# Attention in units of eight slots: scores and maxima in one stretch, projection and rotation behind it, then the unit's own values

## Chip, cores, metric

The kernel runs on one core of a Trainium2 chip. The metric is the device time of one execution in microseconds; of several runs the median counts. The engines are TensorE (PE; its weight loads are PEld), VectorE (DVE), ScalarE (ACT), GpSimd (POOL) and SyncE (SP), which here issues all DMAs. TensorE writes into eight PSUM banks, each of 128 partitions x 512 floats.

## What is computed

A layer of three parts over x of shape (4, 1024, 128): half a routed feed-forward network of eight experts, attention with low-rank query and key paths, and half the same feed-forward network again.

```python
def _reference_tuple_inner(x, w_down_q, w_down_kv, w_up_q, w_up_k, w_up_v, w_out, ln_scale, ln_bias):
    b, s, d = x.shape
    residual = x
    h = (x - mu) * jax.lax.rsqrt(var + LN_EPS) * ln_scale + ln_bias
    c_q = h @ w_down_q.T
    c_kv = h @ w_down_kv.T
    q = (c_q @ w_up_q.T).reshape(b, s, H, DH).transpose(0, 2, 1, 3)
    k = (c_kv @ w_up_k.T).reshape(b, s, H, DH).transpose(0, 2, 1, 3)
    v = (c_kv @ w_up_v.T).reshape(b, s, H, DH).transpose(0, 2, 1, 3)
    q = _apply_rope_subspace(q, DR)
    k = _apply_rope_subspace(k, DR)
    scores = jnp.einsum('bhqd,bhkd->bhqk', q, k) * scale
    attn = jax.nn.softmax(scores, axis=-1)
    out = jnp.einsum('bhqk,bhkd->bhqd', attn, v)
    out = out.transpose(0, 2, 1, 3).reshape(b, s, H * DH)
    out = out @ w_out.T + residual
...
x = x + 0.5 * _L0_ffn_ref(_layernorm(x, axis=-1), ...)
x = x + _L0_attn_ref(_layernorm(x, axis=-1), ...)
x = x + 0.5 * _L0_ffn_ref(_layernorm(x, axis=-1), ...)
```

There are 16 heads of 64. The indices of the top scores are not part of the result.

## The kernel before

**Stages.** The first feed-forward part runs to about 240 us, attention to about 1493 us, then the second feed-forward part. The change lies in the attention loop, in `run`.

**Units and slots.** A pair of heads and half of a batch's queries (512) make a *unit*; there are 64. A unit has eight *slots*, one for each block of 128 keys, 512 slots in all (`NSLOT`). The loop goes over 128 groups of four slots (`NGRP`), and one more to finish.

**Scores.** `score` (L769) makes one slot's scores for one head in four matmuls: three for the product in split precision, the fourth subtracts the row maxima, which stand in `maxr`. Both heads of the pair run next to each other, in the upper and lower 64 rows of the array. The bank is chosen in L779 from five, psS[0] to psS[3] and psX. After the fourth matmul ACT writes the exponential into a tile `p` (L785), of which there are `PBUFS` = 8, and POOL adds the unit's tiles up in `acc` (`accumulate`, L797); `direct` says how many of the last tiles TensorE sums instead.

**Maxima.** `passA` (L744) makes unsplit scores in psA[0] or psA[1] (one for each head), and DVE reduces them (L756). It runs 15 slots ahead (`AHEAD`). `MAXIMA` says before which score of a group each maxima stand. After a unit's sixteenth reduction `max_row` sends the maxima through DRAM to a row.

**Values.** `values` (L799) multiplies the `p` tiles of a slot with the latents `ckn` into psC, in sixteen matmuls for a group; at the unit's last slot ACT copies psC to `osb` (L806). A group does the values of the group before it.

**Denominators and projection.** `den` (L808) sums `acc` over partitions into a bank from `aux`, copies it, and sends it through DRAM to `dT`. `outp` (L827) multiplies `osb` with the folded matrix `G` in banks `bankO` (psX and psS[3]), one bank for each head; `add` in it scales head 0 on ACT (L849), scales and adds head 1 on DVE (L852), and adds head 0 (L854).

**Rotation.** `rope` (L625) makes queries and keys of later pairs in nine stages: fetch the latents, six matmuls into psX and psS[3] ("mm"), five DVE operations ("vector", L660 to L664), two casts on ACT (L672), a subtraction on POOL (L680), two DMAs out.

**Background.** Generators for the next batch's normalization and routing give one step at a time: `step` takes the next whose kind (other, VectorE, TensorE) is allowed at that place. Their PSUM banks come from `aux`, which goes round `rest`: psS[0] and psS[1].

**Order.** The schedule is manual: each engine executes its instructions in the order in which the program makes them. Within a group: the pairs of scores and maxima of both heads in turn; at the tenth pair the due DMAs and a background step; then the matmuls in `halves` (a projection in one group, a rotation in the next), the denominators every second group, the rotation's DVE work, due work ("end"), loads of later pairs, the casts, and the values of the group before, with a background step after the second slot. `at` puts work under a group and a place, `run_later` does it there. All DMAs of the loop stand in SP's queue in the order of issue.

Of the kernel before, what the change touches and what calls it, by code (L numbers as in the profile page):

```python
# [27 lines left out]
AHEAD = 15  # L28
NSLOT = B * 128
NGRP = NSLOT // 4  # L30
PBUFS = 8
MAXIMA = ((3, 8, 13), (0, 5, 10))
OTHER, VECTOR, PE, NEVER = 0, 1, 2, 3
NROPE = 9
ACTS = (4, 6, 7)
# [5 lines left out]

def direct(U):

    return 1 if U % 3 == 2 and U < 56 else 0


class Kernel:
# [494 lines left out]
    def attn_pre(self, b):  # L542
# [15 lines left out]
        def stage(k, h):  # L558
# [30 lines left out]
            elif k in (far[6], far[6] + 1):  # L589
                if k == far[6]:  # L590
                    st["y2", h] = rows4(new("ya2", 2))
                self.norm(st["y2", h], [y[:, i, :] for i in range(4)], mv2[:, q], rstd2[:, q], k - far[6])
            elif k == far[7]:
                ps = self.aux()
                for i in range(4):
                    nc.tensor.transpose(ps[:, i * 128:(i + 1) * 128], st["y2", h][:, i, :], self.ident)
                st["hT", h] = new("hT_a", 0)
                nc.scalar.activation(st["hT", h], ps, AF.Identity, bias=self.lnsb[:, 1:2], scale=self.lnsb[:, 0:1])
            elif k == far[8]:

                pc = self.aux()
                nc.tensor.matmul(pc, self.wdn, st["hT", h], start=True, stop=True)
                st["ckT", h] = new("ckT", 3)[0:64]
                nc.scalar.copy(st["ckT", h], pc[0:64, :])
                C = st["C", h] = self.prep.tile([128, 2, 512], F32R, name="C_a", bufs=2)
                nc.vector.tensor_copy(C[:, 0, :], pc)
                nc.vector.tensor_tensor(C[:, 1, :], pc, self.f(C[:, 0, :]), ALU.subtract)
            elif k == far[8] + 1:
                self.dma(out=self.c_scr[b][h], in_=st["C", h])
                self.latents.add((b, h))  # L610
            elif k == far[9]:
                assert b < 2 or self.slot > 128 * (b - 1)
                pt = self.aux()
                for i in range(4):
                    nc.tensor.transpose(pt[:, i * 64:(i + 1) * 64], st["ckT", h][:, i * 128:(i + 1) * 128], self.ident[0:64, 0:64])
                nc.vector.tensor_copy(self.ckn[b % 2][:, 4 * h:4 * h + 4, :], pt[:, 0:256].rearrange("p (t l) -> p t l", t=4))

        for k in range(far[9] + 1 + far[10]):
# [6 lines left out]
    def rope(self, n, stage):  # L625
# [29 lines left out]
        elif stage == "vector":  # L655
# [4 lines left out]
            nc.vector.tensor_tensor(rt[:, 0:2, :], even.unsqueeze(1).to_broadcast([128, 2, 512]), self.table[:, 1:3, cs], ALU.mult)  # L660
            nc.vector.tensor_tensor(even, odd, self.table[:, 0, cs], ALU.mult)
            nc.vector.tensor_tensor(odd, odd, self.table[:, 1, cs], ALU.mult)
            nc.vector.tensor_tensor(w["eo"][:, 1, :], odd, rt[:, 1, :], ALU.add)  # L663
            nc.vector.tensor_tensor(w["eo"][:, 0, :], even, rt[:, 0, :], ALU.add)  # L664
        elif stage == "sum":
# [133 lines left out]
    def values(self, s):  # L799
        nc = self.nc  # L800
        U, c = divmod(s, 8)
        b = U // 16
        for hh in range(2):
            nc.tensor.matmul(self.psC[64 * hh:64 * hh + 64, :], self.ckn[b % 2][:, c, :], self.p_of[s][:, hh, :], start=c == 0, stop=c == 7)  # L804
        if c == 7:
            nc.scalar.copy(self.osb_of.pop(U), self.psC)  # L806

    def den(self, U):  # L808

        nc = self.nc  # L810
        osb = self.osb_of[U] = self.op2.tile([128, 512], F32, name="osb")
        pd = self.aux()
        parts = [self.p_of[8 * U + c] for c in range(8 - direct(U), 8)] + [self.acc_of[U]]
        for k, part in enumerate(parts):
            for n in range(4):
                nc.tensor.matmul(pd[32 * n:32 * n + 32, 0:256], self.ones, part[:, n // 2, 256 * (n % 2):256 * (n % 2) + 256], start=k == 0, stop=k == direct(U))  # L816
# [6 lines left out]
        last = U == 2 * 8 * B - 1  # L823
        self.at(self.group + 1, lambda: nc.sync.dma_start(out=dT, in_=d1.rearrange("(h x) (y p) -> p (h x y)", x=2, p=128)), "mid")
        self.at(self.group + (4 if last else 3), lambda: self.outp(U, osb, dT), "side")

    def outp(self, U, osb, dT):  # L827

# [27 lines left out]
        self.at(self.group, add)  # L856

    def run(self):
# [4 lines left out]
        self.ready, self.routed, self.done, self.roped, self.latents = set(), set(), set(), set(), set()  # L863
        streams = [[], [], []]

        credit = [0.0] * len(streams)
# [144 lines left out]
        def rope(g, place):  # L1011
            for d, stages in ROPE[place].items():
                n, r = divmod(g - d, 2)
                if r == 0 and 0 <= n and n + NROPE < 16 * B:
                    for stage in stages.split():
                        self.rope(n + NROPE, stage)

        for g in range(NGRP + 1):
            s0 = 4 * g
            self.group, self.slot = g, s0  # L1020
            rope(g, "side")
            self.run_later(g, "side")

            def rows(hh):
                maxima = lambda i: self.passA(s0 + AHEAD + i, hh) if s0 + AHEAD + i < NSLOT else None
                for n in range(16):
# [9 lines left out]
            side = self.halves  # L1038
            for n, pair in enumerate(zip_longest(rows(0), rows(1))):
                for fn in pair:  # L1040
                    if fn:
                        fn()
                if n == 9:
                    rope(g, "mid")
                    self.run_later(g, "mid")
                    step(OTHER)
            self.halves = [[], []]
# [6 lines left out]
            free = g < 16 or g % 2 == 1 or g >= 2 * (16 * B - NROPE) + 2  # L1054
            step(PE if free else OTHER, free)
            if g and g % 2 == 0:
                self.den(g // 2 - 1)
            rope(g, "end")
            self.run_later(g, "end")
            if g == 1 or (g < NGRP and g % 4 == 3):  # L1060
                P = g // 4 + 3 if g > 1 else 2
                if P < NP:
                    for n, fn in enumerate(self.loads(P)):
                        self.at(g + 1 + n // 8, fn, ("mid", "end")[n // 4 % 2])
                if P == NP + 1:
                    self.ffn_weights2(self.QT[a], self.KT[a], self.QT[c])
                    self.dma(out=xs[0], in_=self.x2_scr[0])

            rope(g, "cast")
            for s in range(s0 - 4, s0):  # L1070
                if s >= 0:
                    self.values(s)
                if s == s0 - 3:
                    step(VECTOR, free)
        for i in range(2):
            for k in range(2):
                for hl in range(2):
# [4 lines left out]
        with ExitStack() as ctx:  # L1082
# [5 lines left out]
            g = self.ffn_pre(self.prep, (6, 7), x_of, self.wts2[:, 3].rearrange("p e t -> p t e"), rows=3)  # L1088

            def bg2(n):  # L1090
                for place in ("mid", "side", "end"):
                    self.run_later(NGRP + 1 + n, place)
                    self.both()
                if n >= GS:
# [59 lines left out]
```

## Time and profile before

| what | value |
| --- | --- |
| runs before | 1653.92, 1653.47, 1652.03 us; median 1653.47 |
| span of the profiled execution | 1648.4 us |
| TensorE matmul instructions | 11044 |
| score matmuls into psS / psX (L781, with the row of maxima) | 3584 / 512 |
| values (L804) | 2048 instructions, 468.8 us busy, 600 ns each |
| maxima on DVE (L756) | 1024, 684.8 us busy, 688 ns each |
| exponentials on ACT (L785) | 1024, some 600 ns each |
| sums on POOL (L797) | 430, 872.6 + 152.4 us busy, 2.38 us each |
| copies of psC (L806) | 64, the first at 253.4 us, the last at 1493.0 us |

The copies of psC mark the units: (1493.0 - 253.4)/63 = 19.7 us from one to the next. In a group of instructions the page gives the line, the engine, what it writes and reads, how often, then the time in which at least one was running, the mean length of one, and the idle time of the engine just before. Matmuls overlap one another, so their lengths do not add up; from start to start is the better measure. In the timeline the columns are start, length, engine, line and operation, and in brackets the engine's idle time before and what ended it.

### The profile page before, as it was taken

To read this page: it belongs to the slowest core of one execution; us is meant where nothing else is said; L and a number is where in the kernel's file an instruction comes from. 1 tells how busy PE (TensorE), PEld (TensorE's weight loads), DVE (VectorE), ACT (ScalarE), POOL (GpSimd) and SP (SyncE) were. 2 spreads that over 40 slices of the span, in tenths; PEclk is the share of its full clock that TensorE was granted. 3 is DMA by queue.
4 is the path that set the end of the run, shared out by engine and by line. 5 is a ranking of instruction groups with operands and counts; after the bars stand their busy time and mean duration, and the time that the engine had idled before them with its cause. 6 is when DMAs were issued, how large, how long until landed. Compare 5 with 4: busy or idle time off the path is not lost.

```text
span 1648.4 us, 31237 instructions
## 1 busy us (share of the span) xinstructions
PE 1593.2 (97%) x11044; PEld 1033.2 (63%) x11044; DVE 1317.6 (80%) x2417; ACT 1013.5 (61%) x2220; POOL 1456.0 (88%) x833
## 2 busy tenths in 40 slices
PE   7998989999999999999999999999999999998998
PEld 5876765566566665666565666666566655656776
DVE  6556668888988888888899889889988868616897
ACT  4675666666666666666666656666566655654555
POOL 5668889999999989999999999999999999895676
PEclk9999999999999999999999999999999999999999
DMA  7025557555555655555555556666655532114443
GB/s 226 1 65 166 155 141 168 142 142 130 134 140 140 142 142 134 146 140 138 131 138 142 129 143 152 150 147 141 141 140 149 130 66 53 36 57 138 140 133 103
DMA packets 241149, 212.28 MB, mean 129 GB/s; under 512 B 157664, under 2 KB 170592, under 8 KB 240224
## 3 DMA queue, kind: packets, MB, share of 16 engines
q1 hardware_dynamic: 240992, 210.28, 50.6%
q8 instruction: 87, 1.43, 0.4%
q14 instruction: 70, 0.57, 0.1%
HBM read 130.39 MB, written 79.82 MB: 128 GB/s over the span
## 4 chain that ended last, share of the span: by engine, by line
PE 68%; POOL 3%; DVE 3%; ACT 2%; issue 2%; POOLq 0%; DVEq 0%; ACTq 0%
PE psc L804 24%; PE ps_s L781 21%; PE ps_a L755 6%; PE psx L781 3%; PE ps_s L521 3%; PE ps_s L816 2%; PE psx L476 2%; PE psx L839 2%; POOL acc L797 2%; PE psx L647 2%; ACT p L785 1%; PE ps_s L839 1%; POOL p L529 1%; PE psc L521 1%; DVE m L756 1%
## 5 line engine op out<-in xcount | busy, mean ns | idle before, releaser
L797 POOL TENSOR_TENSOR acc<-acc,p 128x1024 f32<-128x1024 f32 x366 | 872.6, 2384 | 56.3 <-ACT p L785 30.8
L756 DVE TENSOR_REDUCE m<-ps_a 128x1 f32<-128x512 f32 x1024 | 684.8, 688 | 158.0 <-PE ps_a L755 136.2
L785 ACT ACTIVATE p<-ps_s 128x512 f32<-128x512 f32 x896 | 478.2, 602 | 230.7 <-PE ps_s L781 197.1
L781 PE MATMUL ps_s<-QT,KT 64*128 64x512 f32 x2688 | 548.3, 397 | 3.1 <-DVE eo L663 3.0
L804 PE MATMUL psc<-p,ckn 128*64 128x512 f32 x2048 | 468.8, 600 | 0.0
L781 PEld LDWEIGHTS ps_s<-QT,KT 64*128 64x128 f32 x2688 | 351.2, 185 | 138.8 <-issue 76.3
L755 PE MATMUL ps_a<-KT,QT 64*128 64x512 f32 x1024 | 417.9, 419 | 5.0 <-DVE m L756 3.5
L804 PEld LDWEIGHTS psc<-p,ckn 128*64 128x64 f32 x2048 | 135.8, 137 | 257.3 <-issue 252.3
L781 PE MATMUL ps_s<-maxr,one_row 64*128 64x512 f32 x896 | 237.0, 391 | 0.0
L755 PEld LDWEIGHTS ps_a<-KT,QT 64*128 64x128 f32 x1024 | 184.5, 184 | 36.4 <-DVE m L756 12.8
L797 POOL TENSOR_TENSOR acc<-p 128x1024 f32<-128x1024 f32 x64 | 152.4, 2381 | 14.2 <-ACT p L785 11.9
L806 ACT COPY osb<-psc 128x512 f32<-128x512 f32 x64 | 37.6, 587 | 193.3 <-PE psc L804 193.3
L680 POOL TENSOR_TENSOR eo<-eo,hi_r 128x1024 fp32r<-128x1024 f32 x55 | 132.0, 2400 | 0.0
L781 PEld LDWEIGHTS ps_s<-maxr,one_row 64*128 64x128 f32 x896 | 122.3, 185 | 13.5
L781 PE MATMUL psx<-QT,KT 64*128 64x512 f32 x384 | 110.2, 393 | 0.0
L529 POOL TENSOR_TENSOR p<-eo,p 128x512 fp32r<-128x512 f32 x42 | 62.7, 1499 | 40.6 <-ACT p L528 33.1
L425 POOL TENSOR_TENSOR X<-X,dtmp 128x512 f32<-128x512 f32 x54 | 69.1, 1280 | 32.1 <-ACT dtmp L424 31.0
L852 DVE SCALAR_TENSOR_TENSOR X<-ps_s,rT,X 128x128 f32<-128x128 f32 x248 | 68.8, 339 | 26.4 <-PE ps_s L839 26.4
L849 ACT ACTIVATE psx<-psx,rT 128x128 f32<-128x128 f32 x248 | 85.4, 344 | 6.0
L672 ACT CAST hi_r<-eo 128x512 fp32r<-128x512 f32 x128 | 72.9, 615 | 18.8 <-POOL eo L667 14.0
L785 ACT ACTIVATE p<-psx 128x512 f32<-128x512 f32 x128 | 76.9, 601 | 4.4 <-issue 2.1
L781 PEld LDWEIGHTS psx<-QT,KT 64*128 64x128 f32 x384 | 71.1, 185 | 8.5
(237 smaller groups left out, 2388.2 us busy)
## 6 DMA issues: line engine op xcount, KB each, us to landing
C_l<-cs SPq DMA_DIRECT2D x128, 256.0 KB
QT<-qs SPq DMA_DIRECT2D x256, 128.0 KB
KT<-ks SPq DMA_DIRECT2D x256, 128.0 KB
qs<-hi_r SPq DMA_DIRECT2D x32, 512.0 KB
qs<-eo SPq DMA_DIRECT2D x32, 512.0 KB
ks<-hi_r SPq DMA_DIRECT2D x32, 512.0 KB
ks<-eo SPq DMA_DIRECT2D x32, 512.0 KB
rt<-wt SPq DMA_DIRECT2D x52, 256.0 KB
```

The costliest lines, as they stand in the source:

```text
L425: nc.gpsimd.tensor_tensor(X[:, t:t + 4, :], X[:, t:t + 4, :], tmp, ALU.add)
L529: (nc.gpsimd if m < N - 1 else nc.vector).tensor_tensor(sh[:, 1, :], hp, self.f(sh[:, 0, :]), ALU.subtract)
L672: nc.scalar.copy(w["hi"][:, k, :], w["eo"][:, k, :])
L680: nc.gpsimd.tensor_tensor(w["eo"].bitcast(F32R), w["eo"], self.f(w["hi"]), ALU.subtract)
L755: nc.tensor.matmul(self.psA[hh], self.QT[P % 3][r, 0, q0:q0 + 128], self.KT[P % 3][r, 0, kk * 512:kk * 512 + 512], start=True, stop=True)
L756: nc.vector.tensor_reduce(m[0][:, hh, qb, kk:kk + 1], self.psA[hh], AX.X, ALU.max)
L781: nc.tensor.matmul(ps, w, x, start=k == 0, stop=k == 3)
L785: nc.scalar.activation(self.p_of[s][:, hh, :], ps, AF.Exp, scale=0.125)
L797: nc.gpsimd.tensor_tensor(acc, self.p_of[s - 1] if c == 1 else acc, self.p_of[s], ALU.add)
L804: nc.tensor.matmul(self.psC[64 * hh:64 * hh + 64, :], self.ckn[b % 2][:, c, :], self.p_of[s][:, hh, :], start=c == 0, stop=c == 7)
L849: nc.scalar.activation(po[0][:, c], po[0][:, c], AF.Identity, scale=rT[:, i:i + 1])
L852: nc.vector.scalar_tensor_tensor(x, po[1][:, i * 128:(i + 1) * 128], rT[:, 4 + i:5 + i], x, ALU.mult, ALU.add)
```

## The change

The loop goes over 64 units of eight slots instead of 128 groups of four. In a unit:

- Scores and maxima of eight slots stand in one stretch, with new positions in `MAXIMA`. Background steps of kind "other" stand at the pairs 9, 17 and 26 of it, due DMAs at 9, 17 and 26.
- Behind it come the matmuls of the projection and then those of the rotation (`halves`), with the last maxima between them. `bankO` is now psS[1] and psS[2]; the rotation keeps psX and psS[3].
- Then the projection's scaling (both heads on ACT, "scale"), the denominators of the unit before (`den`, in psS[0]), the casts of the rotation before, the DVE work of this rotation, the projection's two sums on DVE, the rotation's sums, its DMAs.
- Then the values of this unit's own eight slots, with background steps after the second, fourth and sixth, and one step that may use TensorE (two in the first eight units). `rest`, the banks for these steps, is now psA.
- `PBUFS` is 10 instead of 8; `direct` is 3 for the last unit, so that TensorE sums its last three tiles. After the loop the last unit's denominators follow.
- The DMA scratch is set to 1024 bytes. L779, which picks a score's bank, is as before.

```diff
-PBUFS = 8
-MAXIMA = ((3, 8, 13), (0, 5, 10))
+NUNIT = NSLOT // 8
+PBUFS = 10
+MAXIMA = ((2, 8, 13, 19, 24, 29), (0, 5, 11, 16, 21, 27))
...
-    return 1 if U % 3 == 2 and U < 56 else 0
+    return 3 if U == NUNIT - 1 else 1 if U % 3 == 2 and U < 56 else 0
...
         if c == 7:
-            nc.scalar.copy(self.osb_of.pop(U), self.psC)
+            osb = self.osb_of[U] = self.op2.tile([128, 512], F32, name="osb")
+            nc.scalar.copy(osb, self.psC)
...
-        pd = self.aux()
+        pd = self.psS[0]
...
+        g = 2 * U + 4
+        self.at(g + (U == NUNIT - 1), lambda: nc.sync.dma_start(out=dT, in_=d1.rearrange("(h x) (y p) -> p (h x y)", x=2, p=128)), "mid")
+        self.at(g + (3 if U == NUNIT - 2 else 2 if U == NUNIT - 1 else 1), lambda: self.outp(U, self.osb_of.pop(U), dT), "side")
...
-            for i in range(4):
-                c = slice(i * 128, (i + 1) * 128)
-                nc.scalar.activation(po[0][:, c], po[0][:, c], AF.Identity, scale=rT[:, i:i + 1])
-            for i in range(4):
-                x = self.X[:, t0 + i, :]
-                nc.vector.scalar_tensor_tensor(x, po[1][:, i * 128:(i + 1) * 128], rT[:, 4 + i:5 + i], x, ALU.mult, ALU.add)
             x = self.X[:, t0:t0 + 4, :]
-            nc.vector.tensor_tensor(x, po[0].rearrange("p (t d) -> p t d", t=4), x, ALU.add)
-
+            for hh in range(2):
+                nc.vector.tensor_tensor(x, po[hh].rearrange("p (t d) -> p t d", t=4), x, ALU.add)
+
+        def scale():
+            for hh in range(2):
+                for i in range(4):
+                    c = slice(i * 128, (i + 1) * 128)
+                    nc.scalar.activation(po[hh][:, c], po[hh][:, c], AF.Identity, scale=rT[:, 4 * hh + i:4 * hh + i + 1])
+
+        self.at(self.group, scale, "scale")
...
-        self.rest, self.rope_banks, self.bankO = self.psS[:2], [self.psX, self.psS[3]], [self.psX, self.psS[3]]
+        self.rest, self.rope_banks, self.bankO = self.psA, [self.psX, self.psS[3]], self.psS[1:3]
...
-        ROPE = {"mid": {2: "dhi"}, "side": {0: "mm"}, "end": {-1: "fetch", 0: "vector", 2: "dlo"}, "cast": {1: "hi0 hi1 lo"}}
+        ROPE = {"mid": {2: "dlo"}, "side": {0: "mm"}, "vector": {0: "vector"}, "add": {0: "add"}, "cast": {1: "hi0 hi1 lo"}, "end": {1: "dhi", -1: "fetch"}}
...
+        for U in range(NUNIT):
+            s0 = 8 * U
+            self.group, self.slot = 2 * U, s0
...
+                for n in range(32):
                     if n in MAXIMA[hh]:
                         yield lambda n=n: maxima(MAXIMA[hh].index(n))
-                    yield lambda n=n: self.score(s0 + n // 4, hh, n % 4) if g < NGRP else None
+                    yield lambda n=n: self.score(s0 + n // 4, hh, n % 4)
                 if hh == 1:
-                    yield lambda: maxima(3)
-                yield from side[hh]
-                if hh == 0:
-                    yield lambda: maxima(3)
+                    yield lambda: maxima(6)
+                for n, fn in enumerate(side[hh]):
+                    if hh == 0 and n == 2:
+                        yield lambda: maxima(6)
+                    yield fn
...
+                yield lambda: maxima(7)
...
                 if n == 9:
-                    rope(g, "mid")
-                    self.run_later(g, "mid")
+                    self.run_later(2 * U, "mid")
                     step(OTHER)
+                if n == 17:
+                    rope(U, "mid")
...
+                    self.run_later(2 * U, "end")
+                    step(OTHER)
+                if n == 26:
+                    self.run_later(2 * U + 1, "mid")
+                    step(OTHER)
+                if n == 32:
+                    self.run_later(2 * U + 1, "side")
+                    rope(U, "side")
...
+            self.run_later(2 * U + 1, "scale")
+            if U:
+                self.den(U - 1)
+            rope(U, "cast")
+            rope(U, "vector")
+            self.run_later(2 * U + 1, "end")
+            rope(U, "add")
+            rope(U, "end")
+            for k in range(8):
+                self.values(s0 + k)
+                if k in (1, 3, 5):
+                    step(VECTOR if k == 5 or U < 8 else OTHER)
             self.nrest = 0
...
+            for _ in range(2 if U < 8 else 1):
+                step(PE)
+        self.run_later(NGRP, "mid")
+        self.den(NUNIT - 1)
```

More of the change, by code (lines that the diff above doesn't have):

```diff
@@ L615, in stage @@
                     nc.tensor.transpose(pt[:, i * 64:(i + 1) * 64], st["ckT", h][:, i * 128:(i + 1) * 128], self.ident[0:64, 0:64])
+                self.keys.add((b, h))
                 nc.vector.tensor_copy(self.ckn[b % 2][:, 4 * h:4 * h + 4, :], pt[:, 0:256].rearrange("p (t l) -> p t l", t=4))
@@ L662, in rope @@
             nc.vector.tensor_tensor(odd, odd, self.table[:, 1, cs], ALU.mult)
+        elif stage == "add":
+            (even, odd), rt = w["ps"], self.rt
             nc.vector.tensor_tensor(w["eo"][:, 1, :], odd, rt[:, 1, :], ALU.add)
@@ L802, in values @@
         b = U // 16
+        assert (b, c // 4) in self.keys
         for hh in range(2):
@@ L805, in values @@
         if c == 7:
-            nc.scalar.copy(self.osb_of.pop(U), self.psC)
+            osb = self.osb_of[U] = self.op2.tile([128, 512], F32, name="osb")
+            nc.scalar.copy(osb, self.psC)
     def den(self, U):
         nc = self.nc
-        osb = self.osb_of[U] = self.op2.tile([128, 512], F32, name="osb")
-        pd = self.aux()
+        pd = self.psS[0]
         parts = [self.p_of[8 * U + c] for c in range(8 - direct(U), 8)] + [self.acc_of[U]]
@@ L815, in den @@
             for n in range(4):
-                nc.tensor.matmul(pd[32 * n:32 * n + 32, 0:256], self.ones, part[:, n // 2, 256 * (n % 2):256 * (n % 2) + 256], start=k == 0, stop=k == direct(U))
+                nc.tensor.matmul(pd[32 * n:32 * n + 32, 0:256], self.ones, part[:, n // 2, 256 * (n % 2):256 * (n % 2) + 256], start=k == 0, stop=k == len(parts) - 1)
         dsb = self.op1.tile([128, 256], F32, name="dsb")
@@ L822, in den @@
         nc.sync.dma_start(out=d1, in_=dsb[0:128:32, :])
-        last = U == 2 * 8 * B - 1
-        self.at(self.group + 1, lambda: nc.sync.dma_start(out=dT, in_=d1.rearrange("(h x) (y p) -> p (h x y)", x=2, p=128)), "mid")
-        self.at(self.group + (4 if last else 3), lambda: self.outp(U, osb, dT), "side")
+        g = 2 * U + 4
+        self.at(g + (U == NUNIT - 1), lambda: nc.sync.dma_start(out=dT, in_=d1.rearrange("(h x) (y p) -> p (h x y)", x=2, p=128)), "mid")
+        self.at(g + (3 if U == NUNIT - 2 else 2 if U == NUNIT - 1 else 1), lambda: self.outp(U, self.osb_of.pop(U), dT), "side")
     def outp(self, U, osb, dT):
@@ L862, in run @@
         self.later, self.m_of, self.acc_of, self.p_of, self.osb_of, self.rope_of = {}, {}, {}, {}, {}, {}
-        self.ready, self.routed, self.done, self.roped, self.latents = set(), set(), set(), set(), set()
+        self.ready, self.routed, self.done, self.roped, self.latents, self.keys = set(), set(), set(), set(), set(), set()
         streams = [[], [], []]
@@ L1006, in step, with rope @@
             return OTHER
-        ROPE = {"mid": {2: "dhi"}, "side": {0: "mm"}, "end": {-1: "fetch", 0: "vector", 2: "dlo"}, "cast": {1: "hi0 hi1 lo"}}
-        def rope(g, place):
+        ROPE = {"mid": {2: "dlo"}, "side": {0: "mm"}, "vector": {0: "vector"}, "add": {0: "add"}, "cast": {1: "hi0 hi1 lo"}, "end": {1: "dhi", -1: "fetch"}}
+        def rope(U, place):
             for d, stages in ROPE[place].items():
-                n, r = divmod(g - d, 2)
-                if r == 0 and 0 <= n and n + NROPE < 16 * B:
+                if 0 <= U - d and U - d + NROPE < 16 * B:
                     for stage in stages.split():
[L1016 to L1022, printed above, removed]
+                        self.rope(U - d + NROPE, stage)
+        for U in range(NUNIT):
+            s0 = 8 * U
+            self.group, self.slot = 2 * U, s0
+            self.halves = [[], []]
+            side = self.halves
             def rows(hh):
                 maxima = lambda i: self.passA(s0 + AHEAD + i, hh) if s0 + AHEAD + i < NSLOT else None
-                for n in range(16):
+                for n in range(32):
                     if n in MAXIMA[hh]:
                         yield lambda n=n: maxima(MAXIMA[hh].index(n))
-                    yield lambda n=n: self.score(s0 + n // 4, hh, n % 4) if g < NGRP else None
+                    yield lambda n=n: self.score(s0 + n // 4, hh, n % 4)
                 if hh == 1:
-                    yield lambda: maxima(3)
-                yield from side[hh]
-                if hh == 0:
-                    yield lambda: maxima(3)
-            side = self.halves
+                    yield lambda: maxima(6)
[3 more added lines that the diff above has]
+                    yield fn
+                if hh == 0 and len(side[hh]) < 3:
+                    yield lambda: maxima(6)
+                yield lambda: maxima(7)
             for n, pair in enumerate(zip_longest(rows(0), rows(1))):
@@ L1043, in run @@
                 if n == 9:
-                    rope(g, "mid")
-                    self.run_later(g, "mid")
+                    self.run_later(2 * U, "mid")
                     step(OTHER)
+                if n == 17:
+                    rope(U, "mid")
+                    if U % 2 == 0:
+                        P = U // 2 + 2
+                        if P < NP:
+                            for k, fn in enumerate(self.loads(P)):
+                                self.at(2 * U + (k // 4 + 1) // 2, fn, ("end", "mid")[k // 4 % 2])
+                        if P == NP + 1:
+                            self.ffn_weights2(self.QT[a], self.KT[a], self.QT[c])
+                            self.dma(out=xs[0], in_=self.x2_scr[0])
+                    self.run_later(2 * U, "end")
[6 more added lines that the diff above has]
+                    rope(U, "side")
             self.halves = [[], []]
@@ L1051, in run @@
                 streams[1].append(pre2(b - 1))
-            self.nrest = 0
[L1054 to L1074, printed above, removed]
+            self.run_later(2 * U + 1, "scale")
[10 more added lines that the diff above has]
+                    step(VECTOR if k == 5 or U < 8 else OTHER)
+            self.nrest = 0
+            for _ in range(2 if U < 8 else 1):
+                step(PE)
+        self.run_later(NGRP, "mid")
+        self.den(NUNIT - 1)
         for i in range(2):
@@ L1090, in bg2 @@
             def bg2(n):
-                for place in ("mid", "side", "end"):
+                for place in ("mid", "side", "scale", "end"):
                     self.run_later(NGRP + 1 + n, place)
@@ L1149 @@
     x = _layout({n: np.asarray(v) for n, v in inputs.items()})
-    nc = bacc.Bacc("TRN2", target_bir_lowering=False, num_devices=1)
+    nc = bacc.Bacc("TRN2", target_bir_lowering=False, num_devices=1, dynamic_dma_scratch_size=1024)
     build(nc)
```

## The prediction

> **What bounds the kernel now.** I read the page's busy shares and its chain first, then the attention stage's busy times, then who makes TensorE wait there, then TensorE's timeline of one unit, then all engines around one change of work. The page and its chain:
>
> ```profile
> PE 1593.2 (97%) x11044; PEld 1033.2 (63%) x11044; DVE 1317.6 (80%) x2417; ACT 1013.5 (61%) x2220; POOL 1456.0 (88%) x833
> ...
> PE 68%; POOL 3%; DVE 3%; ACT 2%; issue 2%; POOLq 0%; DVEq 0%; ACTq 0%
> ```
>
> The changed loop runs from 240 to 1493 us, busy times in the order PE, PEld, DVE, ACT, POOL:
>
> ```profile
> 240.00:1493.00 1253.00, 1238.39 (x9166) 751.90 (x9163) 1037.14 (x1886) 779.30 (x1654) 1176.95 (x547) 1.00 0.54 129
> ```
>
> TensorE works 98.8% of it at full granted clock; POOL stands at 94%, 76 us short. TensorE's waits in that window are (total, times, longest):
>
> ```profile
> PE ps_s L816 <- POOL acc L797: 5.9, 1, 5.9
> PE psx L647 <- ACT p L785: 2.7, 8, 1.1
> PE ps_a L755 <- DVE m L756: 2.2, 5, 0.8
> PE psx L839 <- ACT p L785: 1.5, 5, 0.5
> ```
>
> Some 12 us in 64 units. So the end is set by TensorE's own issue; every microsecond for which its queue is held lengthens the run, and what leaves its queue shortens it. One unit, TensorE alone (start, length):
>
> ```profile
> 1126.72 0.50 PE L781 MATMUL ps_s<-QT,KT 64*128 64x512 f32 x1
> ...
> 1127.06 0.63 PE L781 MATMUL ps_s<-QT,KT 64*128 64x512 f32 x4
> ...
> 1131.22 0.27 PE L839 MATMUL psx<-G,osb 64*128 64x128 f32 x1
> ...
> 1132.44 3.65 PE L804 MATMUL psc<-p,ckn 128*64 128x512 f32 x16
> 1136.02 0.50 PE L781 MATMUL ps_s<-QT,KT 64*128 64x512 f32 x1
> ...
> 1142.12 0.64 PE L816 MATMUL ps_s<-acc,ones 128*32 128x256 f32 x8
> 1142.68 3.66 PE L804 MATMUL psc<-p,ckn 128*64 128x512 f32 x16
> ```
>
> The two heads run side by side, so I count ticks, one for a pair. A half unit has 16 ticks of scores and 3 of maxima before its projection: from the second tick (1127.06) to the projection (1131.22) are 18 ticks in 4.16 us, 0.231 each. The first takes 0.34, because it follows another kind of work. Four slots of values run 3.58 us to the next score (1132.44 to 1136.02). Last, a half where TensorE must wait for an exponential, all engines:
>
> ```profile
> 700.01 0.40 PE L781 MATMUL ps_s<-maxr,one_row 64*128 64x512 f32 x2
> ...
> 700.50 2.07 ACT L785 ACTIVATE p<-ps_s 128x512 f32<-128x512 f32 x4 [3.23 <-PE ps_s L781]
> ...
> 703.20 0.61 ACT L785 ACTIVATE p<-psx 128x512 f32<-128x512 f32 x1
> ...
> 703.68 1.59 ACT L785 ACTIVATE p<-ps_s 128x512 f32<-128x512 f32 x3
> ...
> 703.86 0.50 PE L647 MATMUL psx<-C_l,wup 64*128 64x512 f32 x1 [0.21 <-ACT p L785]
> ...
> 704.20 0.39 PE L647 MATMUL psx<-C_l,wup 64*128 64x512 f32 x1
> ```
>
> Four prices: a slot's first exponential starts 0.49 after its last score matmul (700.01 to 700.50) and takes 0.60; the next follows after 0.48 (703.20 to 703.68); the bank's next writer starts 0.05 after the end (703.81 to 703.86); and after such a wait the second tick comes 0.34 later instead of 0.23, so a restart costs 0.11.
>
> **The change, part by part.**
>
> *One stretch of eight slots.* It does not touch L779: a score's bank is still (2(s mod 4)+head) mod 5. In order, slots 0 to 7 write banks 0,1 | 2,3 | 4,0 | 1,2 | 0,1 | 2,3 | 4,0 | 1,2. Five banks would allow a distance of five; from slot 3 to slot 4 it is three. Before, 3.58 us of values stood between these slots. Now slot 4 follows at once. Let T be the start of slot 3's last matmuls (both heads at tick 18). Head 0's exponential runs from T+0.49 to T+1.09 and frees bank 1 at T+1.14; slot 4's head 1 wants it two ticks after T, at T+0.46 (maxima fill its place in the tick between). Bank 0, due at T+0.23, is free by T+0.46, since slot 2 ended four ticks before; that lies within the same wait. TensorE's queue is in order, so behind the held matmul stand all later scores and maxima, and DVE and POOL behind those. The loss is 1.14 - 0.46 = 0.68, with the restart 0.79. Bounds: 0.5 if ACT's start is quicker, 1.6 if a pair of normalizations (0.78 in ACT's queue) comes just before; such pairs I price apart. 64 units x 0.79 = 51 us.
>
> *Projection right after the stretch, in banks 1 and 2.* These (psS[1:3]) are the banks of slot 7, the last written. T' is its last tick. The projection's head 0 is due at T'+0.23 and gets its bank at T'+1.14: 0.91, plus the restart 0.11. Head 1's bank comes free at T'+0.49+0.48+0.60+0.05 = T'+1.62; its first matmul would follow a doubled tick later (0.24, and the restart) at T'+1.49: 0.13 more. Sum 1.15, for 62 units (the first two have no projection): 71 us. Before, projection and rotation used psX and psS[3], whose exponentials are three or more tiles older; hence only 2.7 and 1.5 us in the waits. Queued behind it are the rotation, the sums for the denominators and all values: nothing on TensorE can fill the hole. Bounds 0.8 (if head 1 is free in time and ACT starts quicker) and 1.9.
>
> The skill's page "Perfetto Trace Analysis", section Matmuls, advises that independent matmul groups rotate through different PSUM banks, so that one's evacuation overlaps the next one's matmuls. The rows at 703 us show what breaking that costs; the rule speaks against both places. The page "ScalarE: Activation LUTs", section What ACT_TABLE_LOAD costs, gives 186 + 0.833 x 512 = 612 ns for such an ACTIVATE and an overlap of 93: start to start 0.52 where the rows show 0.48. By it the sum would be some 4 us higher; the rows decide.
>
> *Fewer changes of work.* One change from scores to values and back falls away per unit. Values run 3.65 - 0.60 = 3.05 us from first to last start, 7 pairs at 0.435; the next score starts 0.53 after the last, 0.09 over, and the second tick is 0.11 late: 0.20. The change into the values gives at most 0.1. I take 0.25: 64 x 0.25 = -16 us. Bounds -25 and 0.
>
> *Background transposes move to banks psA, after the values.* Their drain was covered by 3.58 us of values:
>
> ```profile
> 695.56 0.69 DVE L287 CAST xs<-ps_s 128x512 fp32r<-128x512 f32 x1
> 696.28 0.69 DVE L288 TENSOR_TENSOR xs<-ps_s,xs 128x512 fp32r<-128x512 f32 x1
> ```
>
> The second ends 1.5 us after its transposes; now the maxima of head 0 want that bank 0.57 us into the next stretch. About 1 us for each of 6 such steps, as much or more for 6 of L602 (a copy and two such operations), less for 6 of L596: at most 17, at least 0. I take 12.
>
> *Moved ACT work.* Three of seven background places lie inside the stretch (two of six before). 44 pairs of normalizations at 0.78 run in the window; at 3/7 of them and full loss 15 us, against about 5 lost before (the ACT waits above). I take +5, bounds 0 and 15.
>
> *No lag of values, ten p tiles.* Costs nothing on TensorE: slot 7's p is ready 1.6 us after the stretch, long before its values at some 9 us. POOL has 7 sums of 2.38 and one rounding of 2.40, 19.1 us, in a unit of over 20, and ten tiles let it run late. If that cover went, it would show as waits of L785 on POOL. Splitting the projection's scale and sum puts four more L849 (0.344 each) on ACT and saves DVE four L852 (0.258 apart) less one sum; both run under 7 us of values. The same cover holds the denominators, whose sum for the unit before was finished ten microseconds earlier.
>
> *DMA queue.* The same loads in other places: K and Q of a pair are issued one unit ahead of their first maxima, the maxima's row 15 us before use, the denominators' return a unit before the scale. SP's waits move; TensorE doesn't stand behind them: 0, bounds 0 and 5.
>
> *End.* The last unit gives three tiles to TensorE instead of POOL: the one wait of 5.9 falls away, three times 8 matmuls at some 0.46 are added: -4.5. The last return comes later: +1.
>
> Sum: 51 + 71 - 16 + 12 + 5 - 4.5 + 1 = +119.5. The profiled execution spans 1648.4, so 1768; the median of the runs, 1653.5, lies 5.1 above the span: 1773 us.
>
> **The rivals.**
>
> *Only one of the two bank waits is real* (the other is covered, by later exponentials or an order of issue that I misread). With the first alone 1653.5 + 51 - 16 + 12 + 5 - 3.5 = 1702, with the second alone 1722. For it: the two rest on different banks and orders. Against: both follow from the same rows.
>
> *Faster: POOL sets the pace, and the extra tiles free it.* At 94% it is near its limit, and the lag of four slots with eight tiles may hold it back; TensorE's holes would then be filled by time that it would have waited anyway, and 16 + 4.5 are won: 1633. It decides if the bank waits together stay under 20.5/64 = 0.32 us a unit. Against: TensorE waited for POOL once, 5.9 us, in 64 units.
>
> *The holes spread.* DVE starts the next unit's maxima late, because scale, rotation and sums now all fall behind the values; another 0.9 us a unit: 1830. For it: DVE is 83% busy (1037/1253). Against: a longer unit gives it slack.
>
> *The change does not do what it says*: nothing moves, 1653.
>
> **How the numbers follow.** Forecast, both waits: 0.70, its own range 1706 (lower bounds: 32 + 50 - 25 - 5) to 1834 (both waits a third longer, 163, the small terms at their tops: -16 + 17 + 15 + 5 - 3.5). One wait: 0.11. Faster: 0.09. Spread: 0.08. No change: 0.02. The range 1695 to 1810 takes in both cases of one wait and leaves out the faster case and the tops. A measurement can't tell 0.2% (3.3 us) from no change. Faster 0.09, same 0.02, slower 0.70 + 0.11 + 0.08 = 0.89.
>
> **What would show it.** In the new profile TensorE's waits on L785 should lead: about 0.7 us once in the middle of each stretch, at a score into ps_s, and about 0.9 at each projection matmul; together near 100 us. TensorE's busy share of the stage should fall to about 92%, POOL's to 87%, and units take some 21 us instead of 19.7. The transition from values to scores should be seen 64 times. If the waits on L785 stay under 20 us, the prediction is wrong in its main step; if DVE or POOL lead the list, the fourth case holds.

## The result and the profile after

| | median us | ratio to before, 95% interval |
| --- | --- | --- |
| before, beside these runs | 1653.7 | |
| after the change | 1772.6 | 1.0723 [1.0703, 1.0743] |

The kernel became 7.2% slower. The profiled execution after spans 1770.5 us, 122.1 more than before. Its page (busy time, share of the span and number for each engine, then the chain):

```profile
PE 1649.4 (93%) x11068; PEld 1050.2 (59%) x11068; DVE 1273.4 (72%) x2225; ACT 1096.1 (62%) x2476; POOL 1447.7 (82%) x830
...
PE 12%; ACT 2%; DVE 1%; POOL 1%; issue 1%; DMA 0%; POOLq 0%; SPq 0%; DVEq 0%; ACTq 0%
```

Every engine but ACT (61% to 62%) has a smaller share, and none has come nearer to full; nothing new is the bound. The chain stops early this time (its shares sum to 17%), so it can't be used, and the stage must be read from the waits. The attention stage, now to 1607 us (busy times of PE, PEld, DVE, ACT, POOL, then clock, DMA share, GB/s):

```profile
240.00:1607.00 1367.00, 1287.76 (x9143) 765.09 (x9143) 993.29 (x1707) 859.48 (x1901) 1168.32 (x545) 1.00 0.46 117
```

The stage is 114 us longer. TensorE is busy for 94% of it, POOL for 85%, and the granted clock stays full (1.00). TensorE's waits there (total, times, longest):

```profile
PE ps_s L844 <- ACT p L789: 36.5, 62, 0.8
PE ps_s L785 <- ACT p L789: 19.5, 28, 3.4
PE ps_a L759 <- DVE C_a L608: 9.3, 6, 1.6
PE ps_a L759 <- DVE xs L289: 5.1, 6, 0.8
PE ps_a L759 <- DVE m L760: 4.2, 10, 1.5
PE ps_a L759 <- ACT hT_a L599: 1.2, 6, 0.2
```

The projection (L844) waits for an exponential in each of the 62 units that have one; scores (L785) and, new, maxima behind background transposes follow. This view counts from the modelled end of the last matmul, and leaves short waits out (it has 28 at a score, where 64 stretches have one), so it shows less than is lost: from start to start is the better measure. The middle of one stretch, TensorE and then ACT (start, length):

```profile
731.50 0.40 PE L785 MATMUL ps_s<-maxr,one_row 64*128 64x512 f32 x2
731.98 0.49 PE L785 MATMUL ps_s<-QT,KT 64*128 64x512 f32 x1
731.98 0.50 PE L759 MATMUL ps_a<-KT,QT 64*128 64x512 f32 x1
732.31 1.02 PE L785 MATMUL ps_s<-QT,KT 64*128 64x512 f32 x4
```

Of the four in the last row, the first is head 0's second matmul; the others, seen from 732.5 on, start later:

```profile
732.59 0.74 PE L785 MATMUL ps_s<-QT,KT 64*128 64x512 f32 x3
```

```profile
731.33 1.69 ACT L789 ACTIVATE p<-ps_s 128x512 f32<-128x512 f32 x3
```

The second of these three, slot 3's head 0, by itself:

```profile
731.94 0.60 ACT L789 ACTIVATE p<-ps_s 128x512 f32<-128x512 f32 x1
```

The last scores of slot 3 start at T = 731.50. Slot 4's first matmul (head 0, bank 0) should start at T+0.23 and starts at 731.98, 0.06 after the exponential on its bank ends (731.33 + 0.59); head 0's second comes 0.33 later, not 0.23. Head 1 wants bank 1 at T+0.46. The exponential on that bank runs from T+0.44 to T+1.04, and head 1 starts at 732.59, T+1.09. The end of the same stretch, ACT and then TensorE:

```profile
736.92 0.60 ACT L789 ACTIVATE p<-ps_s 128x512 f32<-128x512 f32 x1
```

```profile
736.43 0.62 PE L785 MATMUL ps_s<-maxr,one_row 64*128 64x512 f32 x2
737.57 0.37 PE L844 MATMUL ps_s<-G,osb 64*128 64x128 f32 x1 [0.52 <-ACT p L789]
```

The last scores start at 736.43 (head 0) and 736.65 (head 1, the second of the two in the row), the projection at 737.57, 0.05 after head 0's exponential (736.92 to 737.52) has left bank 1.

### The profile page after: what moved, and what is told of

It reads as the page before. It is cut to its first block, busy times and chain, and to the rows that moved or that the text cites. A ratio compares the mean times of both kernels' runs of the same rounds, so it can differ in the third digit from the quotient of the medians.

```text
span 1770.5 us, 31129 instructions
## 1 busy us (share of the span) xinstructions
PE 1649.4 (93%) x11068; PEld 1050.2 (59%) x11068; DVE 1273.4 (72%) x2225; ACT 1096.1 (62%) x2476; POOL 1447.7 (82%) x830
## 5 line engine op out<-in xcount | busy, mean ns | idle before, releaser
L785 PE MATMUL ps_s<-QT,KT 64*128 64x512 f32 x2688 | 583.2, 404 | 23.8 <-ACT p L789 20.3
L789 ACT ACTIVATE p<-ps_s 128x512 f32<-128x512 f32 x896 | 479.3, 601 | 120.3 <-PE ps_s L785 114.0
L785 PEld LDWEIGHTS ps_s<-QT,KT 64*128 64x128 f32 x2688 | 368.1, 185 | 144.0 <-ACT p L789 77.2
L809 PE MATMUL psc<-p,ckn 128*64 128x512 f32 x2048 | 453.6, 595 | 0.0
L759 PE MATMUL ps_a<-KT,QT 64*128 64x512 f32 x1024 | 405.3, 428 | 20.8 <-DVE C_a L608 9.3
L785 PE MATMUL ps_s<-maxr,one_row 64*128 64x512 f32 x896 | 273.1, 392 | 0.0
L860 ACT ACTIVATE ps_s<-ps_s,rT 128x128 f32<-128x128 f32 x496 | 164.4, 341 | 79.5 <-issue 67.5
L785 PEld LDWEIGHTS ps_s<-maxr,one_row 64*128 64x128 f32 x896 | 144.2, 185 | 14.8
L844 PE MATMUL ps_s<-G,osb 64*128 64x128 f32 x992 | 101.9, 285 | 36.5 <-ACT p L789 36.5
L844 PEld LDWEIGHTS ps_s<-G,osb 64*128 64x128 f32 x992 | 90.1, 187 | 63.6 <-ACT p L789 63.6
L785 PE MATMUL psx<-QT,KT 64*128 64x512 f32 x384 | 110.2, 391 | 0.0
L854 DVE TENSOR_TENSOR X<-ps_s,X 128x512 f32<-128x512 f32 x124 | 85.1, 686 | 28.4 <-ACT ps_s L860 22.2
```

The costliest lines, as they stand in the source:

```text
L759: nc.tensor.matmul(self.psA[hh], self.QT[P % 3][r, 0, q0:q0 + 128], self.KT[P % 3][r, 0, kk * 512:kk * 512 + 512], start=True, stop=True)
L785: nc.tensor.matmul(ps, w, x, start=k == 0, stop=k == 3)
L789: nc.scalar.activation(self.p_of[s][:, hh, :], ps, AF.Exp, scale=0.125)
L844: nc.tensor.matmul(po[hh][:, i * 128:(i + 1) * 128], osb[r, i * 128:(i + 1) * 128], self.G[r, j, :], start=True, stop=True)
L854: nc.vector.tensor_tensor(x, po[hh].rearrange("p (t d) -> p t d", t=4), x, ALU.add)
L860: nc.scalar.activation(po[hh][:, c], po[hh][:, c], AF.Identity, scale=rT[:, 4 * hh + i:4 * hh + i + 1])
```

## The experiments

All edits are made to the changed kernel. Theory: the two places where a matmul follows too closely on an exponential in the same bank make the loss. Rivals: the moved scale, rotation and sums cost it, or ACT's pace over eight slots.

**1. Five banks in turn through all eight slots.**

```diff
-        ps = (self.psS + [self.psX])[(2 * (s % 4) + hh) % 5]
+        ps = (self.psS + [self.psX])[(2 * (s % 8) + hh) % 5]
```

> The changed kernel with one index altered: a score's bank is (2(s mod 8)+head) mod 5, so that the five banks go round through all eight slots; slot 7 then ends on psX and psS[0], and the projection's banks belong to slots 5 and 6. Bank theory: both waits go, 51 + 71 us, 1773 - 122 = 1651 us, and the TensorE waits on L789 nearly vanish. Rival (the time is lost in the moved scale, rotation and sums, or in the long stretch as such): within 20 us of 1773.

Measured 1667.4 us, 1.0087 [1.0071, 1.0102]: one index takes 105 us of the 119 away; it is 16 us above the expected 1651. Its waits in the attention stage:

```profile
PE ps_s L785 <- ACT p L789: 10.9, 15, 2.9
PE ps_a L759 <- DVE C_a L608: 9.3, 6, 1.6
PE ps_a L759 <- DVE m L760: 5.5, 9, 2.0
PE ps_a L759 <- DVE xs L289: 5.1, 6, 0.9
```

The waits at the projection are gone. The rivals fall: scale, rotation and sums stand where they stood. Some 15 us more than before the change remain, in the transposes' banks among others.

**2. Only the wait behind the stretch taken away.**

```diff
-        self.rest, self.rope_banks, self.bankO = self.psA, [self.psX, self.psS[3]], self.psS[1:3]
+        self.rest, self.rope_banks, self.bankO = self.psA, self.psS[1:3], [self.psX, self.psS[3]]
```

> The changed kernel with the projection in psX and psS[3] and the rotation in psS[1] and psS[2]; scores as they are. Bank theory: only the wait behind the stretch goes (71 us), the one in the middle stays: 1702 us, and a TensorE wait of about 0.7 us at the fifth slot remains. If just one of the two waits is real and it is the one in the middle, 1773; if it is the one behind, 1651 to 1702. Rival (moved work): 1773 within 20.

Measured 1713.9 us, 1.0373 [1.0358, 1.0389]: 59 us less than the change, 46.5 more than experiment 1. No projection waits for an exponential any more; the scores' waits stay as they were in the change:

```profile
PE ps_s L785 <- ACT p L789: 19.2, 29, 3.1
```

**3. Only the wait in the middle taken away.**

```diff
-        ps = (self.psS + [self.psX])[(2 * (s % 4) + hh) % 5]
+        ps = (self.psS + [self.psX])[(2 * (s % 8) + hh + 2) % 5]
```

> The changed kernel with a score's bank at (2(s mod 8)+head+2) mod 5: five banks in turn through the stretch, but slot 7 still on psS[1] and psS[2]. Bank theory: only the wait in the middle goes (51 us): 1722 us, and the projection still waits 0.8 to 0.9 us at each unit. Rival (moved work): 1773 within 20.

Measured 1734.1 us, 1.0499 [1.0481, 1.0516]: 38.5 us less than the change, 67 more than experiment 1. A projection in this run:

```profile
721.34 0.45 PE L785 MATMUL ps_s<-maxr,one_row 64*128 64x512 f32 x2
722.48 0.37 PE L844 MATMUL ps_s<-G,osb 64*128 64x128 f32 x1 [0.69 <-ACT p L789]
```

From the last score's start to the projection 1.14 us. Alone, the two waits cost 46.5 and 67 us, 113.5; together 105. In the changed kernel the wait in the middle leaves the two heads a tick apart up to the end of the stretch: head 1's last score starts 0.22 us after head 0's (median of 62 units; 0.04 in experiment 3). Head 0's exponential, and with it the projection, then comes earlier against the end of the scores: from the last score's start to the projection it is 0.98 us in the mean of the changed kernel, 1.10 in experiment 3, some 7 us in 62 units.

**4. The rotation's matmuls ahead of the projection's**, banks as in the change.

```diff
-                    self.run_later(2 * U + 1, "side")
-                    rope(U, "side")
+                    rope(U, "side")
+                    self.run_later(2 * U + 1, "side")
```

> The changed kernel with the rotation's matmuls ahead of the projection's, banks as they are. Bank theory: three rotation ticks of 0.23 fill the hole ahead of the projection in the 53 units that have both; 1.15 us shrinks to about 0.45 there, 53 x 0.7 = 37 us less: 1736 us. Rival (moved work): the same or slower, since the rotation's DVE work could start earlier but the scale later: 1765 to 1785.

Measured 1735.6 us, 1.0501 [1.0485, 1.0517]: 37 us less. The hole behind the stretch shrinks when other work of TensorE stands in it, with the same banks: from the last score's start to the first value it is 4.13 us in the mean of 62 units of the changed kernel, 3.54 here. Its projection waits:

```profile
PE ps_s L844 <- ACT p L789: 5.4, 9, 0.8
```

The nine left fit the units at the end that have no rotation.

**5. A larger dose in the middle.** Slot 4 follows at a distance of one tile instead of three; the banks behind the stretch are chosen so that nothing waits there, as in experiment 2.

```diff
-        ps = (self.psS + [self.psX])[(2 * (s % 4) + hh) % 5]
+        ps = (self.psS + [self.psX])[(2 * (s % 4) + hh + 2 * (s % 8 // 4)) % 5]
...
-        pd = self.psS[0]
+        pd = self.psX
...
-        self.rest, self.rope_banks, self.bankO = self.psA, [self.psX, self.psS[3]], self.psS[1:3]
+        self.rest, self.rope_banks, self.bankO = self.psA, [self.psS[0], self.psS[3]], self.psS[1:3]
```

> The changed kernel with slots 4 to 7 shifted by two banks, so that slot 4's head 0 follows slot 3's head 1 into psS[2], one tile apart instead of three; the projection in psS[1] and psS[2] (slot 6's), the rotation in psS[0] and psS[3], the denominators in psX, so that nothing waits behind the stretch. To be held against the kernel with only the middle wait (1714 us). Bank theory: the wait at slot 4 grows from 0.68 to T+1.62 - T-0.23 = 1.39 us, 64 x 0.71 = 45 us more: 1759 us. Rival (the middle loses time for another reason, such as ACT's pace over eight slots): 1714 within 15.

Measured 1771.1 us, 1.0716 [1.0692, 1.0739]: 57 us more than experiment 2. The middle of a stretch:

```profile
1036.51 0.42 PE L785 MATMUL ps_s<-maxr,one_row 64*128 64x512 f32 x2
1038.10 0.50 PE L785 MATMUL ps_s<-QT,KT 64*128 64x512 f32 x1 [1.17 <-ACT p L789]
...
1038.44 0.86 PE L785 MATMUL ps_s<-QT,KT 64*128 64x512 f32 x5
```

Slot 4 starts 1.59 us after T, where 1.62 was expected. The excess over the expected 45 us is 12. Most of it goes with the granted clock, which is 0.986 to 0.987 in all five runs here and 0.990 to 0.994 in experiment 2. In six stretches with long waits it stands at 0.50 for 3.4 us or more; one of them, the wait and then the window (columns as for the stage above):

```profile
841.31 0.50 PE L785 MATMUL ps_s<-QT,KT 64*128 64x512 f32 x1 [2.70 <-ACT p L789]
```

```profile
841.80:845.20 3.40, 3.40 (x20) 2.61 (x18) 2.08 (x3) 1.09 (x2) 3.32 (x4) 0.50 0.98 306
```

From slot 3's last score to slot 7's, these six units take 2.0 to 2.3 us more than in experiment 2, some 8 us beyond the others. In 56 units the clock is not lowered there in either run; they take 0.77 us more in the mean, 0.74 in the median, where 0.71 was priced.

**6. Background transposes in psX and psS[3]**, on top of experiment 1.

```diff
-        self.rest, self.rope_banks, self.bankO = self.psA, [self.psX, self.psS[3]], self.psS[1:3]
+        self.rest, self.rope_banks, self.bankO = [self.psX, self.psS[3]], [self.psX, self.psS[3]], self.psS[1:3]
```

> The kernel with banks in turn through eight slots (1667 us) and, besides, the background transposes in psX and psS[3] instead of psA. Theory: TensorE's 15.6 us of waits of L759 on L608, L289 and L599, with their restarts some 16 us, go, since slot 2 and slot 1 want those banks only 1.3 to 2.2 us into the stretch: 1651 us. Rival (the drain merely moves into a wait at a score, or DVE's rotation holds those banks): 1660 to 1667.

Measured 1658.3 us, 1.0030 [1.0017, 1.0044]: 9 us less than experiment 1, not 16. The waits on the transposes' drain are gone, but part came back in another line, which stood at 5.5 us before:

```profile
PE ps_a L759 <- DVE m L760: 13.7, 22, 2.0
```

DVE still works on the drain when the next maxima are due, so the maxima wait for DVE instead of for the bank. The rival was right in part.

**7. The same step behind the fourth slot of values**, on top of experiment 1, banks psA.

```diff
+                if k == 3:
+                    self.nrest = 0
+                    for _ in range(2 if U < 8 else 1):
+                        step(PE)
...
-            for _ in range(2 if U < 8 else 1):
-                step(PE)
```

> The kernel with banks in turn (1667 us) with the background step that may use TensorE moved from behind the values to behind the fourth slot of them; banks psA as in the change. Theory: four slots of values (3.6 us) hide the drain again, some 16 us go; a change of work more for each of 31 such steps costs at most 4: 1651 to 1655 us. Rival (DVE, busy with the rotation, gets to the drain only after the values): 1660 to 1670.

Measured 1655.0 us, 1.0011 [0.9998, 1.0023]: 12 us less than experiment 1, and not to be told from before the change. The values hide the drain for bank and DVE alike.

**8. All background steps out of the stretch**, on top of experiment 6: the three steps behind pairs 9, 17 and 26 stand behind the values of slots 0, 2 and 4.

> As the one with background transposes in psX and psS[3] (1651 expected), with the three background steps of the stretch moved behind the values of slots 0, 2 and 4. Theory: TensorE's 10.9 us of waits of scores on L789, which come from normalizations between the exponentials, go: 1642 us, less than before the change. Rival (ACT then stands behind POOL's seven sums and the next stretch starts late): 1655 to 1675.

Measured 1673.8 us, 1.0117 [1.0098, 1.0136]: 15.5 us more than experiment 6; the time lies where the rival put it. ACT at one unit's end, then TensorE:

```profile
500.10 1.65 ACT L252 ACTIVATE ya<-ya,rstd 128x128 f32<-128x128 f32 x4 [7.65 <-POOL rstd L238]
501.84 0.88 ACT L252 ACTIVATE ya<-X,rstd 128x128 f32<-128x128 f32 x2
502.62 0.56 ACT L812 COPY osb<-psc 128x512 f32<-128x512 f32 x1
503.09 0.88 ACT L252 ACTIVATE ya<-X,rstd 128x128 f32<-128x128 f32 x2
503.87 2.03 ACT L789 ACTIVATE p<-ps_s 128x512 f32<-128x512 f32 x4
```

```profile
504.50 0.79 PE L785 MATMUL ps_s<-QT,KT 64*128 64x512 f32 x1 [6.78 <-ACT p L789]
```

POOL's small step for the normalization now stands behind the unit's sums; ACT waits 7.65 us for it, and the next unit's exponentials wait in ACT's queue, TensorE behind them.

This happens in few units. From one unit's first score to the next one's, units 10, 13, 28 and 29 (from 0) take 4.5 to 8.7 us more than in experiment 6, 27.7 in all; in 28 it is DVE that waits for POOL. In these four the granted clock also stands at 0.50 for 3.4 to 6.8 us each, which is in the 27.7. The 57 units in which neither run's clock is lowered are 13.8 us shorter together: there the theory holds, and four long waits outweigh it.

**9. The last denominators earlier**, on top of experiment 7: behind the last unit's fourth slot of values, their return and the second last projection one or two steps sooner.

```diff
+                    if U == NUNIT - 1:
+                        self.run_later(NGRP, "mid")
+                        self.den(U)
...
-        self.run_later(NGRP, "mid")
-        self.den(NUNIT - 1)
...
-        self.at(g + (U == NUNIT - 1), lambda: nc.sync...
+        self.at(g, lambda: nc.sync...
...
-        self.at(g + (3 if U == NUNIT - 2 else 2...
+        self.at(g + (1 if U == NUNIT - 2 else 2...
```

> The kernel with banks in turn and the background step behind the fourth slot of values (1655 us), with the last unit's denominators behind its fourth slot of values instead of behind the loop, and the last two returns and the second last projection issued one or two steps earlier in the second feed-forward part. Theory: the changed kernel loses about 5.8 us there (its first feed-forward matmul lies 161.3 us before the end, 155.5 before the change), because the weight rows are queued on SP behind the late denominators and both last projections meet in psA: 1650 us, no slower than before the change. Rival (the hand-over is bound by the activation table's load and the first weight rows in any order): 1655.

Measured 1651.8 us, 0.9992 [0.9982, 1.0002]: 3 us less than experiment 7, the same as before the change. In the changed kernel DVE waited for weight rows whose DMAs stand in SP's queue behind the late denominators, and the last projection waited for DVE (SP, DVE, TensorE):

```profile
1609.11 0.49 SPq L827 DMA_DIRECT2D d<-dsb  x1
1609.66 1.86 SPq L469 DMA_DIRECT2D rt<-wt  x4
```

```profile
1614.31 0.69 DVE L536 TENSOR_TENSOR eo<-eo,rt 128x512 f32<-128x512 f32 x1 [2.59 <-DMA rt<-wt]
```

```profile
1620.47 0.48 PE L844 MATMUL ps_a<-G,osb 64*128 64x128 f32 x2 [2.45 <-DVE X L854]
```

From the first feed-forward matmul to the end it was 155.5 us before the change, 161.3 after it, 161.6 in experiment 7, 158.7 here. These are single executions, and not all of the difference is the queue's: in the changed kernel the granted clock stands at 0.50 for 6.8 us of this stretch (from 1621.0), and experiment 1, with the same code there and 3.4 us at that clock, took 159.1.

**10. Nine p tiles**, on top of experiment 9 (`PBUFS` 9).

> The same as the one with the earlier last denominators, with nine p tiles instead of ten. If the extra tiles cost and give nothing on TensorE, as the prediction took it: the same within 3 us. If POOL's pace matters and the tiles are what lets it run late: waits of exponentials on POOL appear, and more than 5 us are lost.

Measured 1651.1 us, 0.9988 [0.9979, 0.9997]. The tenth tile does nothing here, and no exponential waits for a sum on POOL. This is the fastest kernel of the study, 0.1% below before the change, at the edge of what can be told.

## Why the prediction was right

The time fell on the forecast, 1772.6 against 1773, by the mechanism it named. Step by step:

- **The bound.** TensorE's issue set the end, and its holes were added to it. Experiments 1 and 4 show it from two sides: the holes go when the banks are changed, and the one behind the stretch shrinks when other work stands in it, 37 us as worked out.
- **The wait in the middle.** Priced 51 us; alone it costs 46.5, in the changed kernel 38.5 go with it. The order of events is the priced one, to within 0.05 us in the rows above (head 1's start at T+1.09, priced T+1.14).
- **The wait behind the stretch.** Priced 71; alone 67, in the changed kernel 59. The two were added as if independent, and they are not: the first leaves the heads a tick apart and shortens the second. That is some 8 us, and with the small excess in each price the pair measured 105 instead of 122: the over-priced terms of the sum.
- **Fewer changes of work.** Priced 0.25 us a unit. The closest copies of psC in full units lie 18.98 us apart before the change (415.31 and 434.29 us); with the waits away, values start at 442.01 and 460.76 us, 18.75 apart: 0.23.
- **Background transposes.** Priced 12; moved to a better place they give back 12 (experiment 7), to other banks 9.
- **Moved ACT work.** Priced at 5; in experiment 1 the scores' waits for ACT are 10.9 us, of which two, in the second and third unit, take 2.8 and 2.9. ACT waits there for POOL, as in experiment 8. With all three steps out of the stretch, the 57 units of experiment 8 with full clock were 13.8 us shorter, which points to a cost near the prediction's 15 "at full loss"; how much of it stood before the change was not measured.
- **The end.** Priced -4.5 and +1; here the prediction was wrong in sign. The wait of 5.9 us did go, but the hand-over to the feed-forward part is 5.8 us longer, by SP's queue and DVE, which the step on the DMA queue had taken at nothing; a part of the 5.8 may be the clock's (experiment 9). Experiment 9 gets 3 us of it back.
- **No lag, ten tiles.** Taken at nothing; for the tenth tile experiment 10 shows it, the lag was not tested by itself. The rival that POOL sets the pace falls too: at 1651 us POOL does the same work as at 1773.
- **The signs.** In the new kernel's line numbers the exponential is L789. TensorE's waits for it lead the list, as forecast, but the view shows 56 us of them (36.5 + 19.5), not near 100, and 28 waits at scores, not one in each stretch: the view leaves out much of such waits. TensorE's share fell to 94% (forecast 92), POOL's to 85 (87), and units take 21.7 us (21).

The two waits were priced 17 us too high. With both away (experiment 1), 15 us above the kernel before remain, where the other terms were priced at -2.5 together (-16 + 12 + 5 - 3.5), some 17.6 too low. These two errors cancelled: that the total was hit to 1 us is luck, the mechanism is not. The Trainium skill's advice to rotate through PSUM banks ("Perfetto Trace Analysis", section Matmuls) agrees: an index that breaks the rotation once a unit, and a consumer put into the last bank, were worth 105 us.

## What to carry to other kernels

When a loop's stretch gets longer, look at everything that was indexed by the old length: a bank number modulo four slots was harmless only while 3.6 us of other work stood between the fourth slot and the next. Price such a place from the rows: last matmul to start of the evacuation, its length, the release, less the time at which the bank is next wanted, and count the restart. On an engine that sets the end, give the matmuls right behind a stretch the banks that were written longest ago, or put work in front of them.

## What was not expected of the hardware

After a wait the heads, which run side by side in the array, can stay a tick (0.23 us) apart for the rest of the stretch (736.43 and 736.65 us), which made the next wait shorter.

The view of waits showed 36.5 us at the projection, while the kernels with and without these waits differ by 59 to 67 us. The view counts idle time from the modelled end of the last score, 0.39 us after its start (736.65 to 737.04; it shows 0.52 us up to 737.57), while an undisturbed tick follows 0.23 us after the start; and the later restart (0.33 us to the second tick instead of 0.23) is not in it.

A few long waits of TensorE cost more than their length: with the waits of 2.7 to 6.8 us in experiment 8 the granted clock stood at 0.50 for 3.4 or 6.8 us, and the four units grew by 4.5 to 8.7 us.
